# One kernel of attention and convolutions: a check and the squares of the last y in another order on VectorE, and denominators summed eight heads at a time in more places

## The chip, the cores and the metric

The kernel runs on one NeuronCore of a Trainium2 chip, in one launch. The metric is the device time of one execution in microseconds (us). PE is TensorE, DVE is VectorE, ACT is ScalarE, POOL is GpSimd and SP is SyncE; POOL and SP matter here mainly because they issue DMAs, each from a queue of its own that is worked off in order.

## The reference

The input x has the shape (4, 1024, 32, 32), all in float32. Two layers follow each other. Cut to what matters:

```python
# layer 0: attention over the 1024 pixels of an image
qkv = (x @ w_qkv.T + b_qkv).reshape(B, N, 3, 16, 64)
q, k = rmsnorm(rope(q)) * q_norm_w, rmsnorm(rope(k)) * k_norm_w   # over all 1024
attn = softmax(q k^T / 8)                                           # 16 heads, 1024 x 1024 each
y = rmsnorm((attn v) @ w_proj.T) * norm_out_w
x = x + y
# layer 1: bottleneck
out = relu(bn(conv1x1(x, w1)))       # 1024 -> 256, bn over all four images
out = relu(bn(conv3x3(out, w2)))     # 256 -> 256
out = bn(conv1x1(out, w3))           # 256 -> 1024
x = relu(x + softplus(residual_scale) * out)
```

## The kernel before, in words

**Overall.** `program` works through the four images ("batches" b = 0 to 3). For each it projects Q, K and V (`project`, `project2`: a scheme of seven products of quarter matrices in place of eight, so weights need sums that are prepared), turns and normalizes q and k, computes the attention, projects the result to y (`qk_proj` with the weights WP), and normalizes y (`o_norm`, for the last batch `last_norm`). Then come the three convolutions, the first of which begins with batch 1 while batch 3's y is being normalized.

**Who sets the order.** The order of PE and POOL is written by hand, and in the attention and the stages around it that of DVE and ACT too; SP's order is a scheduler's. Small DVE steps are put in by counting: `after(n, step)` runs a step after n products of PE have been issued, `product_done(share)` counts, and steps in `waiting` are taken as time is left over.

**The attention.** `attention(b, c, ...)` runs for two halves of the queries, c = 0 and 1, and in each over eight head pairs hp = 0 to 7. Over both halves pairs are also numbered 0 to 15 below. For each of eight tiles of 128 keys, PE makes the scores of both heads (L791), ACT takes the exponential into `p` (L798), and DVE adds the tiles up (L815 the first two, L817 six more) to `d_`, 128 partitions x 2 heads x 512 queries. PE then makes the context (L826) from the eight tiles of p. `p` has one set of eight tiles, so the next pair's exponentials overwrite what the additions and the context have read.

**Denominators.** The sum over the 128 partitions is made on PE with a matrix of ones.

- By four heads: `sums_of_four` (L895) runs four matmuls for two head pairs. `inverses` copies the result on ACT, writes it to DRAM (L939) and reads it back spread over 128 partitions (L943), DVE takes reciprocals of 128x16 (L955), and `spread` brings the rows back to where the context needs them (L956, L973).
- By eight heads: sums of four head pairs lie in a "home" of 128 x 4 x 512. `halve` folds them with DMAs on POOL's queue: after an even pair the upper half of the partitions is added to the lower (L914, an accumulating DMA); after an odd pair the upper half of its `d_` is copied into the home's upper half (L916) and its lower half is added there (L917, also accumulating, so it follows L916's landing). `sum_of_eight` (L923) then needs one group of four matmuls, with `halves` as the matrix, for four head pairs; then a copy (L925), L939, L943, one reciprocal of 128x32 (L930), L931 and four L973.

Batch 0 sums by four everywhere. Batches 1 and 2 sum by eight in three of their groups of four head pairs and by four in the last. Batch 3 sums by eight in the first half of its queries and by four in the second.

**What uses the inverses.** Batch 0 multiplies on DVE (L905) and adds the bias on ACT (L906) (`mean_and_bias`); the others, and the last pairs of batch 0, use `mean_of_v` (L771 on DVE, L772 on POOL or on DVE).

**What else batch 0 does.** During its attention it prepares weights for the later batches: 21 parts, each loaded by SP (L413 or L390) into a ring of two parts, summed in place by four DVE steps (L416 to L419, or L399 to L402), and stored by four DMAs on POOL's queue (L421 or L404). Two parts stand after the sums of each odd pair, one after those of each even pair. A chunk is loaded again when its store has landed. The even halves of the context are added with a DMA on POOL's queue too (L836).

**The end of layer 0.** The squares of batch 3's y are taken by ACT and added on DVE into `sqy` (L622). `inverse_rms` sums them on PE (`root`, L700, the tile ss_y), then come a square root on ACT (L704), a reciprocal (L709) and two DMAs on POOL (L710, L711), and y is scaled (L997). Between stand the first products of conv1 for batch 1: `conv1_first` (L1057) with DVE's L1075 and the batch statistics (L1032), `t_sums` (L1051), and `go_on`, which continues with `conv1_rest`.

**The check.** All denominators are read back (`dt`, the tile dens_in), and five small DVE steps (L1508 to L1512) find whether one is out of range; a matmul (L1516) makes one number of it. Only if it says so, a second, slower version of the program runs.

Of the kernel before, what the change touches and what calls it, by code (L numbers as in the profile page):

```python
# [11 lines left out]
F32 = mybir.dt.float32  # L12
AF = mybir.ActivationFunctionType
ALU = mybir.AluOpType
# [4 lines left out]
P = 128  # L19
# [66 lines left out]
def program(ctx, tc, x, wblk, w2, w3, vecs, cos, sin, out, bad):  # L86
# [78 lines left out]
    with tc.tile_pool(name=f"st{u}", bufs=2) as st, ExitStack() as s:  # L165
# [608 lines left out]
        def attention(b, c, q_all, k_all, v, probs_, late, ready, extra, slow, steps_in_all, load_parts, fold, then, own):  # L774


            at = half[c]
            sums_, contexts = [], []
            fold_two = 0 < b < B - 1
            homes = fold  # L780
            for hp in range(NHP):
                fold = homes if homes and hp // 4 < len(homes) else None
                n = f"{b}_{c}_{hp}"
                rows = shifts(q_all, k_all, n, hp, c) if bad is None else None
                probs = []
                for t in range(N // P):
                    p = probs_[:, t]
                    sc = bank("sc", f"sc_{n}_{t}")
                    for keys in (low, high):
                        for j, d in enumerate((low, high)):  # L790
                            nc.tensor.matmul(  # L791
                                sc[keys, j], k_all[d, hp, t * P + keys.start : t * P + keys.stop], q_all[d, hp, at],
                                start=True, stop=bad is not None,
                            )
                    if bad is None:
                        for j in range(2):
                            nc.tensor.matmul(sc[:, j], ones[0:1, :], rows[j], start=False, stop=True)
                    nc.scalar.activation(p, sc, AF.Exp)  # L798
                    if t == (3 if b == 0 and (c, hp) != (NCH - 1, NHP - 2) else 1) and late:
                        late.pop(0)()  # L800
                    if t in (5, 6) and biases:
                        biases.pop(0)()
                    if b == 0 and t == 2 and half_done and half_done[0][0] < c * NHP + hp:
                        half_done.pop(0)[1]()
                    if t == 1:
                        if b == 0:
                            d_ = own[hp % 4 // 2][:, hp % 2 * 2 : hp % 2 * 2 + 2, :]
                        elif fold and hp % 2 == 0:
                            d_ = fold[hp // 4][:, hp % 4 // 2 * 2 : hp % 4 // 2 * 2 + 2, :]
                        else:  # L810
                            d_ = acc.tile([P, 2, CH], F32, tag="tot", name=f"den_{n}")
                    if t == 3:
                        load_parts()
                    if t == 1:
                        nc.vector.tensor_tensor(d_, probs[0], p, ALU.add)  # L815
                    elif t > 1:
                        nc.vector.tensor_tensor(d_, d_, p, ALU.add)  # L817
                    probs.append(p)
                if (c, hp) == (NCH - 1, NHP - 1):
                    then()  # L820
                o = bank("cx", f"cx_{n}")
                for t in range(N // P):
                    for j in range(2):
                        h0 = (2 * hp + j) * HD
                        for i, keys in enumerate((low, high)):
                            nc.tensor.matmul(  # L826
                                o[j * HD : (j + 1) * HD, i], v[keys, t, h0 : h0 + HD], probs[t][keys, j],
                                start=(t == 0), stop=(t == N // P - 1),
                            )

                cx = q_all[:, hp, at]
                nc.scalar.copy(cx, o[:, 0])  # L832
                if b == 0 and (c, hp) != (NCH - 1, NHP - 1):
                    other = temp(f"cx_{n}")
                    nc.scalar.copy(other, o[:, 1])
                    nc.gpsimd.dma_start(cx, other, accum_op=ALU.add)  # L836
                else:
                    contexts.append((cx, o[:, 1]))
                if contexts and b == 0:
                    add_context(*contexts.pop(0))  # L840
                if not fold:
                    sums_.append(d_)
                if hp % 2 == min(b, 1) or c == NCH - 1 and (hp == NHP - 1 or fold_two and hp == NHP - 2):
                    for r in ready:
                        if b > 0:
                            mean_of_v(q_all, *r)
                        elif (c, hp) == (NCH - 1, NHP - 1):
                            mean_of_v(q_all, *r, nc.vector)
                        else:
                            mean_and_bias(q_all, *r)  # L850
                    ready.clear()
                if fold:
                    halve(hp, d_, fold[hp // 4][:, hp % 4 // 2 * 2 : hp % 4 // 2 * 2 + 2, :])
                    if hp % 4 == 3:
                        home = fold[hp // 4]
                        eights.append(
                            (c * NHP + hp + 2 - c, lambda n=n, hp=hp, home=home: sum_of_eight(b, c, n, hp, home, ready))
                        )
                if half_done and half_done[0][0] <= c * NHP + hp:
                    half_done.pop(0)[1]()  # L860
                if slow:
                    slow.pop(0)()

                if waiting:
                    next_waiting()
                slots = NCH * NHP - 2
                if extra and steps_in_all == 0 and hp > 0:
                    extra.pop(0)()
                for _ in range(len(extra) - -(-steps_in_all * max(slots - 1 - c * NHP - hp, 0) // slots) if steps_in_all else 0):
                    extra.pop(0)()  # L870
                if contexts and b > 0:
                    add_context(*contexts.pop(0))
                if eights and eights[0][0] <= c * NHP + hp:
                    eights.pop(0)[1]()
                if hp % 2 == 0 or fold:
                    continue
                if (c, hp) == (NCH - 1, NHP - 1):

                    def last(ds=sums_):
                        last_inverses(b, c, hp, n, sums_of_four(n, ds), ready)  # L880

                    if b + 1 < B:
                        after(0.5, last)
                    else:
                        last()
                else:
                    late.append(lambda n=n, hp=hp, ds=sums_: inverses(b, c, hp, n, sums_of_four(n, ds), ready))
                sums_ = []
# [30 lines left out]
        def sum_of_eight(b, c, n, hp, home, ready):  # L919

            dn = bank("sc", f"dn_{n}")[:, 0]
            for i in range(4):
                nc.tensor.matmul(dn[i * QH : (i + 1) * QH, :], halves, home[:, i, :], start=True, stop=True)  # L923
            r = temp(f"rec_{n}")
            nc.scalar.copy(r, dn)  # L925
            k = 2 * ((b * NCH + c) * NHP + hp - 3)
# [132 lines left out]
                    skip_group_check=True,  # L1059
                )  # L1060

        def conv1_first(b, ys, w, between=None):

            o = mine[b] = bank("o1", f"c1_{b}")
            four(o, w[0][0], lambda i: ys[:, i, half[0]], True, False)
            h = temp(f"c11_{b}")
            nc.scalar.copy(h, o)
            product_done()
            if between is not None:
                between()  # L1070
            o2 = bank("o2", f"c1a_{b}")
            four(o2, w[0][1], lambda i: ys[:, i + NH, half[0]], True, True)

# [1 line left out]
                nc.vector.scalar_tensor_tensor(h, o2, col("b1", 0), h, ALU.add, ALU.add)  # L1075
                keep_h1(b, 0, 0, h)

            after(1, done)
            product_done(2 if between is None else 1)

        def conv1_rest(b, ys, w, ss, t1, t2, early=False):

# [251 lines left out]
        for b in range(B):  # L1334
# [61 lines left out]
            probs_ = xp.tile([P, N // P, 2, CH], F32, tag="x", name=f"p_{b}")  # L1396
            fold = [None, None]
            own = None
            if b == 0:
                own = [tp.tile([P, NH, CH], F32, tag=t, name=f"den_{b}_{t}") for t in ("T0", "T2")]  # L1400
            if b > 0:

                fold[0] = homes = [tp.tile([P, NH, CH], F32, tag=t, name=f"den_{b}_{t}") for t in ("T0", "T2")]
                fold[1] = homes[:1] if b + 1 < B else None
            tc_, two = [], []

            def then(b=b, q_all=q_all, tc_=tc_, two=two):
# [69 lines left out]
        back[0] = v_room("back")  # L1477
        read_back(0)
        ss = conv1_sums(w)
        conv1_first(1, back[1], w)  # L1480
        for i in range(0, NH, 2):
            t_sums(back[1], None, t2[i], i, range(3, 4))
        room1, sums2 = t1, t2
# [19 lines left out]
        conv1_first(2, back[2], w, lambda: first_sums_of(2))  # L1503
        for i in range(0, NH, 2):
            t_sums(back[2], None, new[2, i], i, (3,))
        if bad is not None:
            lim = [const.tile([P, 1], F32, name=f"lim{i}") for i in range(2)]
            nc.vector.tensor_reduce(lim[0], dt, AX.X, ALU.min)  # L1508
            nc.vector.tensor_reduce(lim[1], dt, AX.X, ALU.max)
            nc.vector.tensor_scalar(lim[0], lim[0], 1.0 / DEN_MAX, None, ALU.is_ge)  # L1510
            nc.vector.tensor_scalar(lim[1], lim[1], 1.0 / DEN_MIN, None, ALU.is_le)
            nc.vector.tensor_tensor(lim[0], lim[0], lim[1], ALU.mult)  # L1512
        go_on(1, 9)
        if bad is not None:
            o = bank("o2", "fit")
# [575 lines left out]
```

## Time and profile before

| | |
|---|---|
| time, median of 3 runs (lowest, highest) | 2626.78 us (2624.4, 2626.87) |
| the profiled execution's own time | 2627.36 us |
| its span | 2625.6 us |
| mean granted clock of PE in it | 0.996 |
| PE busy | 2598.8 us, 99% |
| DVE busy | 2127.2 us, 81% |
| ACT busy | 1152.4 us, 44% |
| POOL busy | 475.5 us, 18% |

The profile shows one execution. Lines of its timeline begin with the start in us from the beginning of the span and the duration in us, then the engine, the source line, the operation, what it writes and reads, the shapes and the count. A bracket at the end gives the idle time before it on that engine and what ended it. Where a count is over one, the time is that of the group. Matmuls are pipelined, so PE being busy does not say that it runs at its peak; the granted clock says how much of its full speed the throttle let it have. Work on an engine that is idle elsewhere costs nothing unless another engine waits for it.

### The profile page before, as it was taken

The page shows a single profiled execution, that of the slowest core. Times are in us where ns is not written, and L with a number is a line of the kernel's source. Part 1 is how long each engine was busy: PE and PEld are TensorE (multiplying, and loading weights), DVE is VectorE, ACT ScalarE, POOL GpSimd, SP SyncE. Part 2 cuts the span into 40 slices and gives each one's busy share as a digit, 9 for nine tenths or more (in the row PEclk, how much of TensorE's full clock was granted, in tenths as well). Part 3 has the DMA queues.
Part 4 walks back from the last instruction along what each step waited for, and adds up shares of the span by engine and source line. Part 5 has one row for each costly group of instructions (what it writes and reads, how often), then busy time and mean ns, then how long its engine had stood idle before and what let it go on. Part 6 is the DMA issues. An engine that isn't in the chain of part 4 may idle for free. (4 is left out here: it accounts for less than half of the span.)

```text
span 2625.6 us, 40392 instructions
## 1 busy us (share of the span) xinstructions
PE 2598.8 (99%) x15308; PEld 1609.0 (61%) x15308; DVE 2127.2 (81%) x2580; ACT 1152.4 (44%) x1667; POOL 475.5 (18%) x628
## 2 busy tenths in 40 slices
PE   9999999999999999999999999999999999999997
PEld 4448533488888333588887333788885334845843
DVE  5677899998887877888888877988879878878977
ACT  2222466533342556333343565333334655223476
POOL 2541322201011222100011222100112323011000
PEclk9999999999999999999999999999999999999999
DMA  7887888777667443466676452656774643777176
GB/s 280 293 260 200 231 264 262 209 224 234 184 188 213 83 98 74 127 189 223 182 191 174 94 89 55 196 179 198 198 197 109 141 130 106 224 223 226 42 265 239
DMA packets 256010, 478.86 MB, mean 182 GB/s; under 512 B 32320, under 2 KB 125296, under 8 KB 255808
## 3 DMA queue, kind: packets, MB, share of 16 engines
q1 hardware_dynamic: 195440, 287.80, 35.0%
q0 software_dynamic: 52304, 171.61, 26.5%
q10 hardware_dynamic: 8064, 16.78, 1.8%
q8 instruction: 124, 2.03, 0.3%
q14 instruction: 78, 0.64, 0.1%
HBM read 334.77 MB, written 102.25 MB: 166 GB/s over the span
## 5 line engine op out<-in xcount | busy, mean ns | idle before, releaser
L798 ACT ACTIVATE p<-sc 128x1024 f32<-128x1024 f32 x512 | 479.8, 1048 | 17.3 <-PE sc L791 17.0
L791 PE MATMUL sc<-q,k 64*64 64x512 f32 x4096 | 455.2, 591 | 0.6 <-ACT p L798 0.6
L826 PE MATMUL cx<-p,to 64*64 64x512 f32 x3072 | 338.2, 589 | 0.0
L791 PEld LDWEIGHTS sc<-q,k 64*64 64x64 f32 x4096 | 150.6, 132 | 292.8 <-ACT p L798 145.5
L817 DVE TENSOR_TENSOR den<-den,p 128x1024 f32<-128x1024 f32 x192 | 237.9, 1239 | 22.2 <-ACT p L798 2.2
L817 DVE TENSOR_TENSOR den_T<-den_T,p 128x1024 f32<-128x1024 f32 x192 | 236.3, 1231 | 20.4 <-DVE den_T L817 1.4
L826 PEld LDWEIGHTS cx<-p,to 64*64 64x64 f32 x3072 | 117.5, 133 | 212.1 <-issue 211.0
L487 PE MATMUL p_v<-w_v,x 128*128 128x256 f32 x928 | 210.2, 379 | 2.3 <-DVE x L458 2.3
L492 PE MATMUL p_y<-q,w_y 128*128 128x256 f32 x928 | 210.6, 380 | 0.8 <-issue 0.8
L492 PEld LDWEIGHTS p_y<-q,w_y 128*128 128x128 f32 x928 | 175.7, 190 | 30.3 <-issue 5.8
L487 PEld LDWEIGHTS p_v<-w_v,x 128*128 128x128 f32 x928 | 176.0, 190 | 27.8 <-DVE x L458 3.5
L832 ACT COPY q<-cx 128x512 f32<-128x512 f32 x64 | 37.5, 585 | 341.5 <-PE cx L826 341.5
L492 PE MATMUL p_k<-to,w_k 128*128 128x256 f32 x672 | 152.2, 379 | 0.0
L492 PE MATMUL p_q<-to,w_q 128*128 128x256 f32 x672 | 152.2, 379 | 0.0
L492 PEld LDWEIGHTS p_k<-to,w_k 128*128 128x128 f32 x672 | 127.4, 190 | 18.4 <-issue 1.2
L492 PEld LDWEIGHTS p_q<-to,w_q 128*128 128x128 f32 x672 | 127.4, 190 | 18.4 <-issue 1.2
L772 POOL TENSOR_SCALAR q<-q,vec 128x512 f32<-128x512 f32 x42 | 80.3, 1920 | 200.6 <-DVE q L771 200.5
L826 PE MATMUL cx<-p,rq 64*64 64x512 f32 x1024 | 112.7, 589 | 0.0
L1990 PE MATMUL c<-h,w3t 128*128 128x512 f32 x256 | 110.5, 593 | 1.2 <-ACT h L1850 0.7
L734 POOL DMA_DIRECT2D k<-ks x64 | 57.7, 1090 | 182.0 <-ACT p L798 71.2
L492 PE MATMUL p_y<-to,w_y 128*128 128x256 f32 x384 | 90.2, 379 | 0.0
L487 PE MATMUL p_v<-w_v,t 128*128 128x256 f32 x384 | 90.1, 379 | 0.0
(568 smaller groups left out, 4304.8 us busy)
## 6 DMA issues: line engine op xcount, KB each, us to landing
w_v<-wd2f SPq DMA_DIRECT2D x112, 256.0 KB
w_y<-wd2f SPq DMA_DIRECT2D x112, 256.0 KB
w_q<-wd2f SPq DMA_DIRECT2D x84, 256.0 KB
w_k<-wd2f SPq DMA_DIRECT2D x84, 256.0 KB
wd2f<-w_pre POOLq DMA_DIRECT2D x68, 256.0 KB, 3.8
q<-qs POOLq DMA_DIRECT2D x64, 256.0 KB, 5.5
k<-ks POOLq DMA_DIRECT2D x64, 256.0 KB, 4.6
x1df<-y POOLq DMA_DIRECT2D x32, 512.0 KB, 5.8
```

The lines of the kernel that those rows point to most:

```text
L487: nc.tensor.matmul(o[:, q].rearrange("p (g f) -> p g f", g=2), r[:, i, q * P : (q + 1) * P], wt[:, :, i, :], skip_group_check=True, **at,)
L492: nc.tensor.matmul(o[:, q], wt[:, q, i, :], r[:, i, :], skip_group_check=True, **at)
L734: nc.gpsimd.dma_start(dst[i::2, f, :], other[1 - i :: 2, :], accum_op=ALU.add)
L772: engine.tensor_scalar(cx, cx, col("bv", hp), None, ALU.add)
L791: nc.tensor.matmul(sc[keys, j], k_all[d, hp, t * P + keys.start : t * P + keys.stop], q_all[d, hp, at], start=True, stop=bad is not None,)
L798: nc.scalar.activation(p, sc, AF.Exp)
L817: nc.vector.tensor_tensor(d_, d_, p, ALU.add)
L826: nc.tensor.matmul(o[j * HD : (j + 1) * HD, i], v[keys, t, h0 : h0 + HD], probs[t][keys, j], start=(t == 0), stop=(t == N // P - 1),)
L832: nc.scalar.copy(cx, o[:, 0])
L1990: nc.tensor.matmul(os[i], w3t[k][:, f // NH, f % NH, :], h2[b, k][:, half[c]], start=(k == 0), stop=(k == NPT - 1),)
```

## The change

It has three parts.

1. **Batch 0 sums by eight heads** in three of its four groups of four head pairs: pairs 0 to 3 and 4 to 7 of the first half and 0 to 3 of the second. The homes are the tiles T0 and T2. Pairs 4 to 7 of the second half still go by four: 4 and 5 lie in T2 (`own`), 6 and 7 in tiles of their own. The multiplications by the inverses (L905), which came in two for two head pairs, now come in four for four; those of the third group are made at the end of the second half's pair 6 with L771 and L772 on DVE.
2. **Batch 3's second half** sums its first four head pairs by eight. The home consists of two tiles that held the tables of cosines and sines.
3. **The check and the squares.** The five check steps move from after the additions of batch 2's conv1 to between the first two products of batch 1's `conv1_first`, and the step L1075 comes one product later (`lag`), by two additional counts of `product_done` before `t_sums`. In DVE's order the check, the additions of squares (L622) and L1075 now stand ahead of the two additions of `t_sums` (L1051), where before L1075, the statistics and both L1051 stood ahead of four L622.

On PE three groups of four matmuls (128x512) go in batch 0 and one in batch 3. POOL's queue gets 18 DMAs of 256 KB in batch 0 (L914 after the even pairs; L916 and L917 after the odd pairs, behind L836 and ahead of the stores L404 and L421) and 6 in batch 3. The rest of PE's order is as before.

```diff
-            fold_two = 0 < b < B - 1
+            fold_two = True
...
                     if t == 1:
-                        if b == 0:
-                            d_ = own[hp % 4 // 2][:, hp % 2 * 2 : hp % 2 * 2 + 2, :]
+                        if own and c == NCH - 1 and hp in (4, 5):
+                            d_ = own[hp % 2]
                         elif fold and hp % 2 == 0:
-                            d_ = fold[hp // 4][:, hp % 4 // 2 * 2 : hp % 4 // 2 * 2 + 2, :]
+                            d_ = fold[hp // 4][hp % 4 // 2]
...
-                        elif (c, hp) == (NCH - 1, NHP - 1):
+                        elif c == NCH - 1 and hp >= NHP - 2:
                             mean_of_v(q_all, *r, nc.vector)
...
-                halve(hp, d_, fold[hp // 4][:, hp % 4 // 2 * 2 : hp % 4 // 2 * 2 + 2, :])
+                halve(hp, d_, fold[hp // 4][hp % 4 // 2])
...
-                nc.tensor.matmul(dn[i * QH : (i + 1) * QH, :], halves, home[:, i, :], start=True, stop=True)
+                nc.tensor.matmul(dn[i * QH : (i + 1) * QH, :], halves, home[i // 2][:, i % 2, :], start=True, stop=True)
...
-        def conv1_first(b, ys, w, between=None):
+        def conv1_first(b, ys, w, between, lag=1):
...
-            if between is not None:
-                between()
+            between()
...
-            after(1, done)
-            product_done(2 if between is None else 1)
+            after(lag, done)
+            product_done()
...
-            if b == 0:
-                own = [tp.tile([P, NH, CH], F32, tag=t, name=f"den_{b}_{t}") for t in ("T0", "T2")]
-            if b > 0:
-
-                fold[0] = homes = [tp.tile([P, NH, CH], F32, tag=t, name=f"den_{b}_{t}") for t in ("T0", "T2")]
-                fold[1] = homes[:1] if b + 1 < B else None
+            homes = [tp.tile([P, NH, CH], F32, tag=t, name=f"den_{b}_{t}") for t in ("T0", "T2")]
+            fold[0] = homes = [[t[:, i : i + 2, :] for i in (0, 2)] for t in homes]
+            fold[1] = homes[:1]
+            own = homes[1] if b == 0 else None
+            if b == B - 1:
+                fold[1] = [[tp.tile([P, 2, CH], F32, tag=t, name=f"den_{t}") for t in ("cos", "sin")]]
...
-        conv1_first(1, back[1], w)
+        lim = [const.tile([P, 1], F32, name=f"lim{i}") for i in range(2)] if bad is not None else None
+
+        def limits():
+            if bad is not None:
+                nc.vector.tensor_reduce(lim[0], dt, AX.X, ALU.min)
+                nc.vector.tensor_reduce(lim[1], dt, AX.X, ALU.max)
+                nc.vector.tensor_scalar(lim[0], lim[0], 1.0 / DEN_MAX, None, ALU.is_ge)
+                nc.vector.tensor_scalar(lim[1], lim[1], 1.0 / DEN_MIN, None, ALU.is_le)
+                nc.vector.tensor_tensor(lim[0], lim[0], lim[1], ALU.mult)
+
+        conv1_first(1, back[1], w, limits, 2)
+        for share in (1, 0.5):
+            product_done(share)
...
-        if bad is not None:
-            lim = [const.tile([P, 1], F32, name=f"lim{i}") for i in range(2)]
-            nc.vector.tensor_reduce(lim[0], dt, AX.X, ALU.min)
...
```

More of the change, by code (lines that the diff above doesn't have):

```diff
@@ L1505, in program @@
             t_sums(back[2], None, new[2, i], i, (3,))
-        if bad is not None:
-            lim = [const.tile([P, 1], F32, name=f"lim{i}") for i in range(2)]
-            nc.vector.tensor_reduce(lim[0], dt, AX.X, ALU.min)
[L1509 to L1512, printed above, removed]
         go_on(1, 9)
```

## The prediction

> **What bounds the kernel now.** I read the page's first section, then PE's waits, then the timelines of the three places that the diff touches.
>
> ```profile
> PE 2598.8 (99%) x15308; PEld 1609.0 (61%) x15308; DVE 2127.2 (81%) x2580; ACT 1152.4 (44%) x1667; POOL 475.5 (18%) x628
> ```
>
> PE is busy for 99% of the span, so only two things can save time: less PE work, or less of its 27 us of idling. The waits view says who owns the idling:
>
> ```profile
> PE ss_y L700 <- DVE sqy L622: 3.5, 1, 3.5
> PE p_v L487 <- DVE x L458: 2.3, 3, 1.1
> ```
>
> One wait is the largest: PE stands 3.5 us for the last sum of squares of batch 3's y, and nothing else costs over 2.3. PE's timeline there, and the granted clock of 2317–2321 and 2321–2327.5 beside a stretch of batch 0 (columns: PE, PEld, DVE, ACT, POOL busy, clock, DMA share, GB/s):
>
> ```profile
> 2313.67 3.60 PE L1057 MATMUL c<-t,c_S 128*128 128x512 f32 x8
> 2320.81 1.08 PE L700 MATMUL ss_y<-sqy,ones 128*32 128x256 f32 x8 [3.55 <-DVE sqy L622]
> 2321.82 6.04 PE L1057 MATMUL c1s<-to,c_S 128*128 128x512 f32 x8
> ```
>
> ```profile
> 340.00:395.00 55.00, 55.00 (x515) 18.47 (x508) 52.09 (x59) 36.01 (x45) 16.35 (x28) 1.00 0.88 267
> 2317.00:2321.00 4.00, 0.45 (x5) 0.22 (x8) 3.35 (x5) 2.10 (x4) 0.00 (x0) 0.84 0.98 381
> 2321.00:2327.50 6.50, 6.50 (x16) 2.58 (x11) 1.75 (x1) 1.50 (x2) 0.83 (x2) 0.57 0.02 5
> ```
>
> The eight matmuls that follow the stall took 6.04 us, those before it 3.60, and the clock stood at 0.57. The trace's clock record puts the drop 2.5 us after PE stopped and holds it at half for 6.8 us. So the stall costs 3.55 and, for the 5.76 us of work done at half speed, another 2.88: 6.4 in all.
>
> The first window matters too: in batch 0 PE has no gap, but DVE is busy 52.1 of 55 us and the DMA engines 0.88. What is put there has little room.
>
> **Part A, the reordered check and squares.** DVE's order at the stall:
>
> ```profile
> 2315.33 2.34 DVE L1051 TENSOR_TENSOR x<-x,t 128x1024 f32<-128x1024 f32 x2
> 2317.59 3.07 DVE L622 TENSOR_TENSOR sqy<-sqy,sq_y 128x512 f32<-128x512 f32 x4
> ```
>
> Four additions of squares stand behind two additions that only conv1 needs later. The change puts the five limit operations (0.68+0.67+0.45) where DVE now idles 2.1 us, then the additions of squares, with L1075's step and its statistics between them, and the two L1051 last. By the rows: limits 2311.8–2313.5, two L622 to 2314.7, L1075 and statistics to 2316.0, two L622 to 2317.3. PE arrives at 2317.2. The check's input landed at 2307.4, so the limits wait for nothing, and freeing its buffer early releases an ACT square. L1051's outputs now come some 2 us later; their reader is the second group of matmuls behind ss_y. I take 0.2 left: −6.2. Bounds: −6.4, and −2 if the squares' chain itself is late by 2.
>
> **Part B, batch 3's second half.** One group of four matmuls fewer; six copies on POOL's queue, six inverse rows regrouped. Price of a group, from batch 0, where PE is full on both sides:
>
> ```profile
> 314.20 3.61 PE L791 MATMUL sc<-q,k 64*64 64x512 f32 x32
> 317.75 1.06 PE L895 MATMUL dn<-den_T,ones 128*32 128x512 f32 x8
> ```
>
> A head pair without a group takes 13.75 us and one with it 14.90: 1.15 per group. The eight-head group at a boundary costs the same 1.15, except once, in batch 1, where it took half a microsecond more because its second copy (L917) had just landed. By POOL's queue batch 3's new group stands alike (copy issued 2173.5, landed 2177, PE there at 2176.3), so −1.15+0.45 = −0.7. Bounds −1.15 and 0. On SP four DMAs of inverse rows now stand behind two loads of w_y, and on POOL two L772 behind three stores; both queues have idle time there and the readers come a head pair later, so nothing; a readers' wait of up to 0.5 is inside the upper bound. ACT loses three copies and four biases in batch 0; at 44% busy that is worth nothing.
>
> **Part C, batch 0.** Three groups fewer of eight: −3 × 1.15 = −3.45 of PE work. Against that stand 18 copies of 256 KB on POOL's queue (L914, L916, L917). Batch 0 also prepares weights: after an odd head pair's sums DVE makes two parts, POOL stores each in four DMAs, and SP reloads the freed chunk once its store has landed.
>
> ```profile
> 373.59 0.69 DVE L399 TENSOR_TENSOR w_pre<-w_pre,w_pre 128x512 f32<-128x512 f32 x1
> ...
> 389.46 0.68 DVE L399 TENSOR_TENSOR w_pre<-w_pre,w_pre 128x512 f32<-128x512 f32 x1
> ```
>
> ```profile
> 376.02 2.14 POOL L404 DMA_DIRECT2D wd2f<-w_pre  x4 [2.06 <-DMA inv<-densf]
> ```
>
> ```profile
> 380.05 4.71 SPq L390 DMA_DIRECT2D w_pre<-wdf  x6
> ```
>
> Call E the end of the odd pair's sums (373.57). Store at E+2.45, reload issued at E+6.5, the next part's last chunk landed at 388.07 (E+14.5; 14.3 to 15.3 over four rounds), used at E+15.9. Slack: about one microsecond. The change puts L916 and L917 ahead of those stores, and L917 waits for L916's landing. Batch 1 shows that wait:
>
> ```profile
> 995.17 0.55 POOL L916 DMA_DIRECT2D den_T<-den  x1 [10.70 <-DVE den L817]
> 998.34 0.80 POOL L917 DMA_DIRECT2D den_T<-den  x1 [2.62 <-DMA den_T<-den]
> 998.88 1.13 POOL L1390 DMA_DIRECT2D x1df<-in_x_dram  x1
> ```
>
> From L916 to the next DMA is 3.7 us; so the first store goes at about E+4.1, 1.65 later, and the reload lands at about E+16.65 (16.0 to 17.0). The even pairs' L914 is one DMA and stands behind the pair's own L836; it waits only for sums that are done, so I price it at nothing, and at 0.5 per pair if its issue delays the four stores that follow.
>
> DVE meanwhile is ready earlier: two parts (5.56) and nine-microsecond sums (9.11) bring it to E+14.67, where before a pair of L905 (1.2) came first. The four L905 now come together, at the ends of pairs 8 and 12 (ready E+17.07: covered). At pairs 4, 6 and 10 DVE waits: 2.0, and 1.6 twice, where a reciprocal (0.35) comes first; I add 0.5 for the start at pair 2. Sum 5.7.
>
> Does DVE's lateness reach PE? Per four pairs DVE now has 4×9.11 + 6×2.78 + 2.4 + 0.35 = 55.9 us against PE's 4×13.75 + 1.15 = 56.15, so it wins nothing back. The probabilities' buffer lets DVE lag some 13.5 us behind the scores; it lags 8.6 now, so nothing stops within the loop. It shows at the end:
>
> ```profile
> 516.68 1.07 PE L895 MATMUL dn<-den_T,ones 128*32 128x512 f32 x8
> ```
>
> ```profile
> 505.43 7.87 DVE L817 TENSOR_TENSOR den_T<-den_T,p 128x1024 f32<-128x1024 f32 x6
> ```
>
> Before, the last sums ended at 513.2, 3.5 ahead of this group. Now PE comes at 513.2, and pair 14 has four L771/L772 on DVE (4 × 1.13) instead of a pair of L905. DVE without any wait still ends at 512.8–513.3; with 5.7 us of waits at about 518.9. So PE stands 5.7 us. By the conv1 rows a stall drops the clock after 2.5 us for 6.8, of which 3.6 us fall on work: +1.8. C = −3.45 + 5.7 + 1.8 = +4.05. Bounds: −3.45 (loads in time) and +13 (rival two).
>
> The Trainium skill, "TensorE: Matmul & The Clock Gate", section "Part 1: The HAM clock gate", has the clock halved only after one whole idle window of about 3.4 us on a free-running counter. This trace dropped it 2.5 us into a 3.55 us idle, so the measurement decides; by the rule a 5.7 us stall would hold a whole window two times in three, and without the drop the sum is 1.8 lower.
>
> **Sum.** −6.2 − 0.7 + 4.05 = −2.85 on the profiled execution's 2627.36, so 2624.5. That execution lies 0.6 above the median, so 2623.9. About 0.2% (5.25 us) is what a measurement here can tell from no change: this is "same".
>
> **Rivals.**
>
> *The cover holds.* Loads land 14.3 to 15.3 us after E now; if the stores' delay were taken up by the DMA queue and the loads came in time, DVE would wait for nothing and C is −3.45: total −10.4, 2616.4. For it: the stores' landing takes 3.8 us whether they leave together or not, and SP's loads pass 6 at a time, so the last chunk may be set by the stream and not by the first store. Against: the load was issued at 380.05, right when the first store landed (379.99).
>
> *Slower: the DMA engines set the loads.* The share is 0.88 already and the 18 copies, 4.7 MB in some 220 us, add 21 GB/s to 267. If each reload lands 1.8 us later still (E+18.45), all five pairs wait: 3.8 + 2×3.4 + 2×1.4 = 13.4, with the clock (2.9): −6.2−0.7−3.45+13.4+2.9 = +5.9, 2632.7. Each 0.1 us of extra delay costs 0.5 over the five waits; the kernel gets slower than before at all from about 0.6, and by 5.25 from about 1.7.
>
> *The stall at ss_y stays.* ACT's squares wait for a buffer, A gives only −2: total +1.3, 2628.
>
> **How the numbers follow.** Likeliest case 0.42 (its own range 2620 to 2628: waits of 3 to 8 us, clock drop or not); cover holds 0.30; DMA-bound 0.22; stall stays 0.06. Faster by over 0.2%: 0.30, and 0.11 of the likeliest case, whose waits may be under 4 us: 0.41. Slower: most of the third case, and 0.02 of the first: 0.19. Same: 0.40. The range goes from 2615.5, below the cover case, to 2631.5, leaving out about a sixth.
>
> **What would show it.** In conv1, ss_y without an idle before it and the c1s group near 3.6 us. In batch 0, POOL's L917 with waits near 2.6 ahead of L404; DVE's L399 at pairs 4, 6 and 10 waiting for a load, 1.5 to 2 us each; and dn_1_7's group with 4 to 7 us of idle and a lower clock behind it. If that group has no idle, the cover case is right and I am wrong on the stores; if idle is spread over the loop, or over 10 us, the DMA case is. In batch 3, one group of L895 fewer and an L923 with about 1.6 us.

## The result, and the profile after

The changed kernel takes 2652.6 us (median of 5 runs, 2650.44 to 2653.28) against 2626.78 us: a ratio of 1.0098, with a 95% interval of 1.0087 to 1.0109. It is 26 us slower; "same" was forecast, 2623.9, with a range that ended at 2631.5. The profiled execution took 2651.14, its span is 2649.0.

The page's first section and PE's waits (engine, what it waited for, total us, times, longest):

```profile
PE 2603.3 (98%) x15276; PEld 1604.9 (61%) x15276; DVE 2128.4 (80%) x2580; ACT 1152.5 (44%) x1659; POOL 492.0 (19%) x652
```

```profile
PE sc L791 <- ACT p L798: 9.5, 13, 4.2
PE dn L923 <- DVE w_pre L402: 5.5, 1, 5.5
PE dn L895 <- DVE den_T L817: 4.7, 1, 4.7
...
PE ss_y L700 <- DVE sqy L622: 0.5, 1, 0.5
```

The wait that was 3.5 us has shrunk to 0.5, and three new ones stand above it. All three lie in batch 0's attention: scores, an eight-head group, a four-head group. (Small waits that the kernel before has too stand between them and ss_y.)

**Where the time went.** Matching PE's instructions of the two traces one to one gives the offset of the changed kernel at each place. At the first scores of batch 0 it is −0.4 us, at the first product of batch 0's y +27.9, at that y's sum of squares +28.7. From there to batch 3's y it falls to +27.2 (batches 1 to 3 together −1.5). Past the sum of squares ss_y of batch 3 it is +21.3, so conv1 gave back 5.9. The span ends at +23.4: another 2.1 come after the last engine has finished.

**Conv1**, PE's timeline:

```profile
2340.84 3.60 PE L1057 MATMUL c<-t,c_S 128*128 128x512 f32 x8
2344.90 0.64 PE L700 MATMUL ss_y<-sqy,ones 128*32 128x256 f32 x8 [0.46 <-DVE sqy L622]
2345.47 3.70 PE L1057 MATMUL c1s<-to,c_S 128*128 128x512 f32 x8
```

The idle before ss_y is 0.46 instead of 3.55, and the group behind takes 3.70 instead of 6.04: the clock stays up. DVE's order is the forecast one, with L1051 last.

**Batch 0**, two of its stretches, before and then after (PE, PEld, DVE, ACT, POOL busy, clock, DMA share, GB/s):

```profile
395.00:450.00 55.00, 55.00 (x512) 18.53 (x508) 51.64 (x58) 34.96 (x44) 16.20 (x28) 1.00 0.88 262
450.00:515.00 65.00, 65.00 (x601) 22.03 (x594) 58.85 (x63) 40.81 (x52) 14.32 (x25) 1.00 0.78 232
```

```profile
395.00:450.00 55.00, 48.61 (x428) 15.00 (x424) 42.04 (x46) 31.26 (x37) 14.97 (x24) 0.97 0.91 248
450.00:515.00 65.00, 52.62 (x446) 15.65 (x440) 51.83 (x57) 31.23 (x37) 19.57 (x32) 0.97 0.89 246
```

PE, which had no gap, is idle for 6 of 55 and 12 of 65 us, and DVE, which was busy for 51.6 and 58.9 in the same stretches, now for 42.0 and 51.8: both wait. What DVE waits for stands in brackets in its timeline:

```profile
400.28 0.69 DVE L399 TENSOR_TENSOR w_pre<-w_pre,w_pre 128x512 f32<-128x512 f32 x1 [4.01 <-DMA w_pre<-wdf]
...
418.69 0.69 DVE L399 TENSOR_TENSOR w_pre<-w_pre,w_pre 128x512 f32<-128x512 f32 x1 [3.65 <-DMA w_pre<-in_wblk_dram]
...
436.03 0.69 DVE L399 TENSOR_TENSOR w_pre<-w_pre,w_pre 128x512 f32<-128x512 f32 x1 [2.95 <-DMA w_pre<-wdf]
```

These are the parts after pair 6, the second part after pair 7, and the part after pair 8. In all, DVE waits for weights nine times in batch 0's attention, 33.8 us; before, once, 3.5 us. The 30.2 us more are about as much as PE lost there: 28.2 us net, and 3.45 us more for the three groups that it no longer makes, together 31.7. From its first long waits on DVE set the pace, and nearly all that it waited reached PE.

PE feels it inside the loop and not at the end:

```profile
424.14 6.27 PE L791 MATMUL sc<-q,k 64*64 64x512 f32 x40 [4.17 <-ACT p L798]
...
490.54 1.92 PE L923 MATMUL dn<-den_T,halves 128*32 128x512 f32 x4 [5.48 <-DVE w_pre L402]
...
544.52 1.07 PE L895 MATMUL dn<-den,ones 128*32 128x512 f32 x8
```

The scores of pair 9 wait for exponentials, and these for DVE, which has not yet read pair 8's tiles of p. The third eight-head group waits 5.48 us; the releaser that the view names had long been at work, and the copy L917, issued at 486.94, landed at 490.45, 0.09 us before PE went on. The last group, where the whole stall was forecast, has no idle before it.

**POOL and SP**, after pair 5 is the first of these rows and after pair 7 the second (their sums ended at 381.26 and 412.18):

```profile
384.79 0.84 POOL L917 DMA_DIRECT2D den_T<-den  x1 [2.61 <-DMA den_T<-den]
385.34 4.59 POOL L404 DMA_DIRECT2D wd2f<-w_pre  x8
...
412.55 0.55 POOL L916 DMA_DIRECT2D den_T<-den  x1 [6.73 <-DVE den L817]
419.35 0.83 POOL L917 DMA_DIRECT2D den_T<-den  x1 [6.25 <-DMA den_T<-den]
419.90 4.57 POOL L404 DMA_DIRECT2D wd2f<-w_pre  x8
```

```profile
405.37 3.51 SPq L973 DMA_DIRECT2D inv<-densf  x4
408.99 2.07 SPq L390 DMA_DIRECT2D w_pre<-in_wblk_dram  x4
```

After pair 5 the store goes 4.1 us after the sums, as forecast. After pair 7 it goes 7.7 us after: eight DMAs of SP (four inverse rows, four reloads) went out just before L916, whose landing takes 6.5 us and not 2.9. The stores, which came in two fours as DVE finished each part, now leave as a block of eight. Over batch 0's attention a reload took 5.0 us from issue to landing before (median of 67), and takes 7.1 now (68).

### The profile page after: what moved, and what is told of

It is laid out like the page before. It is cut to its first block, busy times and chain, and to the rows that moved or that the text cites. A ratio compares the mean times of both kernels' runs of the same rounds, so it can differ in the third digit from the quotient of the medians.

```text
span 2649.0 us, 40339 instructions
## 1 busy us (share of the span) xinstructions
PE 2603.3 (98%) x15276; PEld 1604.9 (61%) x15276; DVE 2128.4 (80%) x2580; ACT 1152.5 (44%) x1659; POOL 492.0 (19%) x652
## 5 line engine op out<-in xcount | busy, mean ns | idle before, releaser
L791 PE MATMUL sc<-q,k 64*64 64x512 f32 x4096 | 461.6, 596 | 10.2 <-ACT p L798 9.5
L817 DVE TENSOR_TENSOR den<-den,p 128x1024 f32<-128x1024 f32 x228 | 281.4, 1234 | 26.7 <-ACT p L798 2.7
L817 DVE TENSOR_TENSOR den_T<-den_T,p 128x1024 f32<-128x1024 f32 x144 | 177.6, 1233 | 15.0
L772 POOL TENSOR_SCALAR q<-q,vec 128x512 f32<-128x512 f32 x42 | 78.7, 1882 | 174.7 <-DVE q L771 174.7
```

What stands on the lines that cost most here:

```text
L772: engine.tensor_scalar(cx, cx, col("bv", hp), None, ALU.add)
L791: nc.tensor.matmul(sc[keys, j], k_all[d, hp, t * P + keys.start : t * P + keys.stop], q_all[d, hp, at], start=True, stop=bad is not None,)
```

## The experiments

Thirteen kernels, one of them twice, were timed beside the kernel before, whose median was 2625.8 to 2626.6 in these comparisons.

### The parts alone

`conv1_only` has the third part alone, `conv1_b3` the third and the second, `b0_only` the first alone.

```diff
 # conv1_b3 against the changed kernel: batch 0 as before
-            fold_two = True
+            fold_two = b > 0
-            own = homes[1] if b == 0 else None
+            if b == 0:
+                own = homes        # fours everywhere, no fold
 # conv1_only: also fold[1] = None for b == 3
 # b0_only: fold_two = b < B - 1, conv1_first and the check as before
```

> The kernel before with the third part of the change alone (check and squares reordered). If the stall at the last sum of squares and the half clock behind it were the whole price, 5.9 us go (the offset measured between the two traces at that place): about 2621. A rival says that in the changed kernel the stall went for another reason, since everything arrives 27 us later there and the back rows and y's squares stand otherwise: then under 3 us are gained here.

> As conv1_only, with batch 3's second half summed by eight as well, batch 0 as before. By the offsets of the changed kernel's trace batch 3's part is worth 0.2 to 1 us: about 2620.5. By the price of a group alone 1.15 more than conv1_only: 2619.9. If its copies on POOL's queue or the inverse rows on SP delay someone, it is slower than conv1_only.

> The kernel before with batch 0 summed by eight in three groups, nothing else changed. If batch 0 is the only place that loses, +28 to +32 us: about 2656. If the parts disturb each other, less.

Measured: conv1_only 2621.49 (ratio 0.9984, interval 0.9975 to 0.9993), conv1_b3 2621.3 (0.9985, 0.9976 to 0.9994), b0_only 2652.27 (1.011, 1.0094 to 1.0125). Conv1's part is worth 4.7 us (1.8 to 6.6 by the interval), which agrees with the 5.9 of the trace. Batch 3's part adds nothing that can be measured; its group, in the trace of conv1_b3:

```profile
2174.25 1.05 PE L923 MATMUL dn<-den_cos,halves 128*32 128x512 f32 x4
2174.90 1.05 PE L923 MATMUL dn<-den_sin,halves 128*32 128x512 f32 x4
2175.88 7.10 PE L791 MATMUL sc<-q,k 64*64 64x512 f32 x64
```

From its start to the next scores are 1.63 us, half a microsecond over a group's 1.15, as forecast. In the same trace and in that of the change PE also idles 0.75 us before the first product of batch 3's y; in the kernel before and in conv1_only it doesn't. The view names no releaser, and what PE waits for stays open, but the wait uses up the 0.7 us that were forecast. And batch 0 alone makes the whole loss.

### Without the copies, and with one group

```diff
 # no_copies
-                    halve(hp, d_, fold[hp // 4][hp % 4 // 2])
+                    if b > 0:
+                        halve(hp, d_, fold[hp // 4][hp % 4 // 2])
 # one_group: only pairs 0 to 3 of batch 0 by eight
+            if b == 0:
+                own = homes
+                fold = [homes[:1], []]
```

> The changed kernel without the DMAs of L914, L916 and L917 in batch 0 (18 of 256 KB); the sums of batch 0's folded groups are then incomplete, everything else is as in the changed kernel. Theory one, the copies hold POOL's stores back and crowd the DMA engines: the 29 us of batch 0 fall to under 10, the reloads land some 15 us after the odd pair's sums, time about 2628 or less. Theory two, the four inverse rows (L973) that now stand ahead of reloads on SP's queue, and the pairs of L905 that no longer cover a reload: the loss stays above 15 us, time over 2638.

> The changed kernel with only one of batch 0's groups by eight (pairs 0 to 3), the others by four as before. It has a third of the copies. If each group costs alike (29 us over three): about 2631. If DVE's small slack takes up the first delays and only their sum reaches PE, less than a third: 2621 to 2627.

Measured: no_copies 2622.76, one_group 2630.23. Taking the 18 copies away takes 29.8 us away, so theory one holds: the copies make the loss, not the regrouped inverses on SP or L905 in fours. In that trace one of the late waits is left, 1.30 us at pair 11's second part:

```profile
458.63 0.69 DVE L399 TENSOR_TENSOR w_pre<-w_pre,w_pre 128x512 f32<-128x512 f32 x1 [1.30 <-DMA w_pre<-in_wblk_dram]
```

But no_copies has three groups fewer on PE than conv1_b3, 3.45 us, and is 1.5 us slower. By their traces PE comes 2.4 us earlier to the first product of batch 0's y and there waits for DVE, whose last sums end at 513.4 and not earlier than conv1_b3's (512.7); at that y's sum of squares 0.3 us of the lead are left:

```profile
511.86 1.99 PE L492 MATMUL p_y<-q,w_y 128*128 128x256 f32 x8
513.79 1.07 PE L896 MATMUL dn<-den,ones 128*32 128x512 f32 x8
516.68 1.99 PE L492 MATMUL p_y<-q,w_y 128*128 128x256 f32 x8 [1.82 <-DVE q L902]
```

So even without the copies' price, work taken from PE brings next to nothing here, because DVE ends no sooner. (Some two microseconds more go at the end of the program; see the last section.)

One group costs 8.9 us over conv1_b3, a little under a third of the 31.3 of three: hardly any slack takes up the first delays. A single wait carries much of it:

```profile
PE dn L895 <- DVE den_T L817: 4.8, 1, 4.8
```

### The place of the copies and their size

The copies do two things: they hold POOL's queue ahead of the stores, and they move 4.7 MB. `behind` issues L916 and L917 after the pair's eight stores, `small_copies` leaves them in place but cuts them to 8 of 512 columns, `behind_small` does both. The six L914 stay where the change put them, behind the even pairs' sums; they were never moved by themselves, so their share isn't known (in the changed kernel they land after 7.5 to 8.0 us from pair 2 on).

```diff
 # behind
+                if fold and b == 0 and hp % 2 == 1:      # after the pair's stores
+                    halve(hp, d_, fold[hp // 4][hp % 4 // 2])
 # small_copies
+                    cut = slice(0, 8 if b == 0 else CH)
+                    halve(hp, d_[:, :, cut], fold[hp // 4][hp % 4 // 2][:, :, cut])
```

> The changed kernel with L916 and L917 of batch 0 issued behind the pair's eight stores on POOL's queue, not ahead of them: the traffic of the copies stays, the holding of the stores goes. If the hold is what costs (first stores 4.1 to 9.2 us after the odd pair's sums in the changed kernel, 2.45 before), most of the 28 us between the changed kernel and the one without copies goes: 2625 to 2632. If the copies' load on the DMA engines costs by itself, reloads still take 9 us from issue to landing, and the time stays over 2640.

> The changed kernel with batch 0's copies cut to 8 of 512 columns (so its folded sums are incomplete), in the same places of POOL's queue: L917 still waits for L916's landing, about 2 to 2.6 us, but the copies move almost nothing. If the hold costs: over 2640. If the load costs: near the kernel without copies, 2623 to 2630. My forecast priced the hold at 1.65 us per store and 5.7 us in all, which alone would give about 2630.

> The changed kernel with batch 0's copies behind the stores and cut to 8 of 512 columns (its folded sums are incomplete): no hold and almost no traffic, but the same waits and places in the queues. If the traffic is what made the third group's copies late (PE idle for 14.3 us) and the reloads slow, the time falls from 2641.3 to near the kernel without copies, 2623 to 2628. If the place behind the stores makes them late whatever their size, PE still idles over 8 us at the third group and the time stays over 2633.

Medians in us:

| batch 0's copies | ahead of the stores | behind them |
|---|---|---|
| full size | 2652.6 (the change) | 2641.32 |
| 8 columns | 2636.6 | 2626.49 |
| none | 2622.76 | |

Both theories were half right. The place costs 11.3 us with full copies and 10.1 with small ones; the traffic costs 16.0 ahead of the stores and 14.8 behind; small copies behind the stores still cost 3.7. The sum of 3.7, 10.1 and 16.0 is the 29.8. (Eight of small_copies' ten times lie between 2635.1 and 2638.6, two at 2627.0 and 2628.5.)

POOL in small_copies, after pair 7, shows the hold with hardly any bytes: the first store goes 5.6 us after the first copy, for whose landing POOL stood 4.34:

```profile
407.16 0.63 POOL L917 DMA_DIRECT2D den_T<-den  x1 [6.72 <-DVE den L817]
412.13 0.99 POOL L918 DMA_DIRECT2D den_T<-den  x1 [4.34 <-DMA den_T<-den]
412.76 4.66 POOL L404 DMA_DIRECT2D wd2f<-w_pre  x8
```

(L917 and L918 there are L916 and L917 of the change.) Reloads took 6.3 us in the median, with next to no traffic added; that points to the stores leaving in eights, which wasn't tried by itself. With the copies behind, the median is back at 4.8 at full size too, though single reloads are late (DVE waits 6.50 us after pair 7 and 4.45 after pair 11), and PE meets the third group before its copies have landed (behind, then behind_small):

```profile
473.10 1.05 PE L926 MATMUL dn<-den_T,halves 128*32 128x512 f32 x4
488.50 1.92 PE L926 MATMUL dn<-den_T,halves 128*32 128x512 f32 x4 [14.34 <-DVE w_pre L399]
```

```profile
474.49 1.92 PE L928 MATMUL dn<-den_T,halves 128*32 128x512 f32 x4 [6.39 <-DVE w_pre L399]
```

In behind, POOL issued L916 at 478.0 and L917 at 484.6, which landed at 488.4: behind eight stores, the copies are late themselves.

### The inverse rows on SP, and two groups

`rows_later` takes batch 0's first two groups' reciprocals one pair later, so that SP has the reloads before the rows; `behind_rows_later` does it in behind. `two_behind` sums only the first half of the queries by eight, so that there is no third group; `two_behind_rows_later` and `two_behind_small` are its variants.

```diff
 # rows_later
-            half_done.append((c * NHP + hp + 3 - c, invert))
+            half_done.append((c * NHP + hp + 3 - c + (1 if b == 0 and c == 0 else 0), invert))
 # two_behind, on top of behind
+            if b == 0:
+                own = homes
+                fold = [homes, []]
```

> The changed kernel with the reciprocals of batch 0's first two groups taken one head pair later, so that on SP's queue the four inverse rows (L973) stand behind the reloads of pairs 7 and 11 and not ahead of them. In the changed kernel DVE waited 3.65 and 5.30 us for those two reloads, and L917 6.25 and 7.16 us behind L916 at the same pairs. If the burst of rows and reloads is what delays both, some 9 us of waits and as much of the stores' delay behind it go: 2636 to 2645. If the copies alone do it, no change from 2652.6 by more than 2.

> Both remedies: copies behind the stores, rows behind the reloads. DVE's waits of 6.5 and 4.5 us at pairs 7 and 11 of the kernel with copies behind the stores should go, and with them 8 to 11 us of its 2641.3: 2630 to 2634, which is still over the 2621 of the kernel with batch 0 as before, since the copies' traffic stays. If the rows don't matter: 2641.

> The changed kernel with two of batch 0's groups by eight (both of the first half of the queries), copies behind the stores; the second half goes by four as before, so there is no third group that PE could meet before its copies have landed (14.3 us of PE's idle in the kernel with all three and copies behind the stores). If the copies' traffic itself is cheap and that wait was the price: about 2621 plus what DVE waits at pairs 7 and 11 (6.5 and 4.5 before) hand on, 2622 to 2630. If the traffic costs by itself, two thirds of its 18 us stay: 2633 or more.

> As two_behind, with the first two groups' reciprocals one pair later, so that the inverse rows stand behind the reloads on SP's queue. If three causes (copies ahead of stores, rows ahead of reloads, PE meeting the third group's copies) are the whole price of summing by eight here: 2618 to 2623, level with the kernel that leaves batch 0 as it was (2621.3) or 2 us under it. If traffic costs by itself, 2628 or more.

> The kernel with batch 0 as before and the other two parts of the change, on the same chip as the two others for the comparison: 2621 again, within 1.5.

> The kernel with two groups and copies behind the stores, the copies cut to 8 columns. It is 5.6 us over the kernel with batch 0 as before (2622.2). If the copies' traffic is what is left, 2620 to 2623; if it is the order on SP's queue or the waits themselves, 2626 to 2628.

Measured: rows_later 2647.23, behind_rows_later 2639.95, two_behind 2627.81, two_behind_rows_later 2631.4, conv1_b3_again 2622.21, two_behind_small 2623.49.

The burst on SP's queue is a small part of the price: 5.4 us in the changed kernel, 1.4 with the copies behind, where 8 to 11 had been expected. It is what made L916 land late after these pairs, though. In rows_later L917 waits 2.65 us after pair 7 and 2.94 after pair 11, where it waited 6.25 and 7.16:

```profile
415.50 0.83 POOL L917 DMA_DIRECT2D den_T<-den  x1 [2.65 <-DMA den_T<-den]
```

DVE's waits of 3.65 and 5.30 us are gone there too, but others grew, and it still waits 30.1 us in all. With two groups the later rows cost more than they bring (3.6 us); DVE then waits for them:

```profile
482.92 1.29 DVE L908 TENSOR_TENSOR q<-q,inv 128x512 f32<-128x512 f32 x2 [5.58 <-DMA inv<-densf]
```

Two groups with the copies behind the stores are 5.6 us over conv1_b3_again, of which 4.3 are the copies' traffic (two_behind_small, whose folded sums are incomplete); what I had hoped for there, a gain of 2 us, isn't to be had. The best version is the one that leaves batch 0 alone: conv1_b3 and conv1_only, 4 to 5 us under the kernel before.

## Why the prediction was wrong

**Part A was right.** −6.2 was forecast; the offset at conv1 moved by 5.9, and conv1_only is 4.7 us under the kernel before (1.8 to 6.6). What was missed is that 0.46 us of idle stay, not 0.2.

**Part B was right within what can be measured**: −0.7 forecast, nothing seen. The half microsecond at its group was there; the 0.75 us before the first product of y, priced at nothing, were there too.

**Part C failed**, at its term "Sum 5.7": DVE waited 30.2 us more, not 5.7. Step by step:

- "The first store goes at about E+4.1" held after pairs 3, 5 and 9 (4.1 to 4.2) and failed after pairs 1, 7 and 11 (9.2, 7.7 and 8.6), where L916's landing took 6.5 to 7.6 us. The 2.62 us were taken from one row of batch 1, with the DMA engines 0.41 busy around it (990 to 999 us); here SP's rows and loads stood in front, and with the rows moved (rows_later) the wait is 2.65 again.
- "The reload lands at about E+16.65": after pairs 3, 5 and 9 DVE went on at E+18.7 to 19.0, after pairs 7 and 11 at E+23.9 and 23.4. I moved the landing by the store's delay alone and left a reload at its old duration. It went from 5.0 to 7.1.
- "The four L905 … covered": not after pair 8 (2.95) nor pair 12 (0.80).
- The second parts of pairs 1, 7 and 11, and pair 2 (5.93, 3.65, 5.30 and 3.13 us, of which 3.5 were there before) were priced at 0.5 together. I had followed one reload of each round and not the other.
- "Nothing stops within the loop" was worked out for 5.7 us of lateness; with 30 the scores stopped for 1.7 us at pair 8 and for 4.2 at pair 9.
- "−3 × 1.15 = −3.45 of PE work" stood in the sum and in the lower bound. Without the copies (no_copies) it doesn't show: DVE's last sums end no sooner, and PE waits for them.
- The 2.1 us at the end of the span were in no term.
- A wait of PE for the copies themselves, priced at 0.45 for batch 3, was not thought of for batch 0's third group. It was 5.48.

**The rivals.** The second named the right mechanism, 1.8 us of extra landing; 2.1 were measured. Its 2632.7 fell short for the same reason: it knew five waits, and there were nine. Its chance was 0.22. "The cover holds" rested on the stores' landing staying at 3.8; it is 4.2 in the page's list of DMA issues, and DVE's nine waits show that the delay wasn't taken up. "The stall stays" fell.

The row that should have warned was in the text: DMA engines 0.88 busy, DVE 52 of 55, a microsecond of slack. A chain of store, landing and reload that has one microsecond to spare, on engines near their full share, does not lengthen by the added piece only.

## What to carry to other kernels

Price a DMA put into a busy queue by the chain that it delays, and at the durations of that place, not of a quiet one: the same copy took 2.9 us where little else was in flight and up to 7.6 behind another queue's burst. Follow every transfer of a round through a shared ring, since the one you leave out can be the late one. And an engine that is 95% busy with slack of one microsecond passes on every wait: three matmul groups saved (3.45 us) were paid for with 30 us. Ask first, too, whether the engine that is spared sets the pace: here DVE did, and without the copies the groups saved next to nothing.

## What the runs showed of the hardware

**The clock falls for whole multiples of 3.41 us.** In the clock records, the drop that runs into the end of the program aside: 6.83 us in the kernel before (stall of 3.55), three times 3.41 in the changed one (4.17, 5.48 and 4.71), 6.83 in one_group (4.79), 13.65 in behind (14.34). One drop of the changed kernel began at 425.15, a microsecond after PE had resumed. The Trainium skill, "TensorE: Matmul & The Clock Gate", section "Part 1: The HAM clock gate", gives a free-running window of 3413 ns, and these lengths agree. So do the places: wherever one of the 16 traces has several drops, they begin a whole number of such windows apart (in the changed kernel 64.85 and 23.89 us, which is 19 and 7). A stall's length alone does not tell its price: 3.55 us of idle had a longer drop than 5.48. What counts in these traces is how much of a window PE is idle. After the first 20 us, the clock fell at the end of all 27 such windows at full clock with 1.99 us or more of PE's idle and of none with 1.94 or less; once down, it came back after a window with 0.54 or less and stayed down with 0.67 or more. A whole idle window was not needed.

**Copies ahead of POOL's stores slow loads on SP's queue.** Reloads issued by SP took 7.1 us (median) with full copies ahead of the stores, 6.3 with small ones there, 4.8 with full copies behind the stores, 5.0 without. The Trainium skill, "DMA: Bandwidth & Descriptors", section "Issuing engines are not separate DMA queues", says that DMAs of all issuing engines end on the same 16 engines. That SP's burst makes POOL's copy land 3.6 us later, and that the copies' traffic costs 15 to 16 us at either place, would fit that. But the place counts as well: behind the stores the same traffic leaves the median load as it was.

**Two microseconds at the end.** From the last instruction of ACT to the end of the span are 5.9 to 6.3 us in nine of the 16 profiles (the kernel before, conv1_b3, b0_only and one_group among them) and 7.8 to 8.0 in the other seven, the changed one among them. In these SP stands some 2 us between two semaphore waits behind the last branch. All seven have three groups by eight in batch 0 with the new conv1. Why was not tried and stays open. It is 2 of the 31.3 us between conv1_b3 and the change, and more than the 1.5 us by which no_copies is slower than conv1_b3.
